# A top-2 mixture of experts computed from 128-token blocks of its chosen experts, in a fused four-layer kernel

## The chip, the cores and the metric

The program runs on one core of a Trainium2 chip. Its time is device microseconds for one execution of the whole program; three executions of the kernel before gave 5038.87 us as the median, with 5027.98 and 5039.68 at the ends. A change of the time counts here relative to that median.

## The reference, cut to what matters

The input `x` has 128 sequences of 32 tokens and 128 channels, so 4096 tokens. Twelve sublayers follow each other (L0 to L3, each a cross-attention, an attention and a feed-forward part), and each adds its result to `x`. The change is in the third one, the feed-forward part of L0, a mixture of eight experts:

```
x = x + _L0_ffn_ref(_layernorm(x, axis=-1), L0_ffn_w_router, L0_ffn_w_up, ...)
    logits = jnp.einsum('bsd,ed->bse', x, w_router)
    top_logits, idx = jax.lax.top_k(logits, K)                      # K = 2 of 8
    router_weights = jax.nn.softmax(top_logits, axis=-1)
    h = jnp.einsum('eud,bsd->bseu', w_up, x) + b_up[None, None]     # u = 512
    h = jax.nn.gelu(h, approximate=False)
    y = jnp.einsum('edu,bseu->bsed', w_down, h) + b_down[None, None]
    y_k = jnp.take_along_axis(y, idx[..., None], axis=2)
    out = jnp.einsum('bskd,bsk->bsd', y_k, router_weights)
```

The reference computes every expert for every token and then keeps two of the eight results of each token, weighted by a softmax of the two best router logits.

## The kernel before, in words

**Tiling.** The tokens are held in SBUF for the whole program as eight groups `X[0]` to `X[7]` of 512 tokens, each a tile of 128 partitions by 4 by 128 channels. All data are float32. Matmul results go to PSUM; ScalarE (ACT), VectorE (DVE) and GpSimd (POOL) work on them. The build fixes one order of instructions for each engine, close to the order in which the Python code emits them; at run time each engine goes through its list in sequence and stops at an instruction whose inputs or buffers aren't ready. The same holds for the queue of SyncE (SP), which issues nearly all the DMAs.

**The feed-forward part.** `L0_ffn` (L770) goes through the groups in chunks (0,1), (2,3), (4,5), (6), (7). For a chunk, `L0_ffn_chunk` (L783) normalizes the tokens, transposes them to `xT` (channels on partitions), computes the router's logits, takes maxima and their indices (L800, L801) and makes from them `R`, a weight of each of the eight experts for each token (`top_weights`; zero for the six experts not chosen). It adds the weighted `b_down` with the small matmuls `pbd`. Then, for each group and each of the eight experts, it computes all 512 tokens: four matmuls `pu` of 128x512 (L815), four Gelu activations into `Hh` (L816), sixteen matmuls `py` of 128x128 (L820), and `add_weighted` (L827), four vector instructions that add `R` times `py` to `X[g]`. That makes 64 passes of one expert over one group. The weights of all experts are in SBUF, in the tile `w_L_ffn`.

**Work beside it.** The attention part of L0 solves, for each token group, a batch of small 32x32 linear systems. It is spread over the neighbours of the feed-forward part by three queues of generators: `kq` builds the kernel matrices of a group (matmuls `kc`, results stored to DRAM as `phik` and `zd`), `sq` solves the systems on DVE (L702 and L703 load the matrices `A`, L707 to L726 eliminate; the result leaves as `yd`), and `oq` forms the output (L743 loads `Y`, then matmuls `ko`) and marks the group as ready for the feed-forward part. A fourth queue `dq` holds the whole of layer L1 for groups 0 and 1 (its own 16 experts have matmuls `ph` at L1087 and `py` at L1095). After each expert pass `side_steps(3, 5.5)` takes three steps of `kq`, 5.5 us worth of `sq`, and one step each of `oq` and `dq`. A chunk doesn't start before all of its groups are ready; the last solve, that of group 7, runs during the chunks (2,3) and (4,5). When the feed-forward part is done, the rest of `dq` is worked off, and the rest of L1 and L2 begins (`L2_xattn` of group 0 is its first part).

Of the kernel before, what the change touches and what calls it, by code (L numbers as in the profile page):

```python
# [9 lines left out]
FP = mybir.dt.float32  # L10
I32 = mybir.dt.int32
U32 = mybir.dt.uint32
AF = mybir.ActivationFunctionType
# [31 lines left out]
def _blocks(d):  # L45
# [18 lines left out]
                    ("temp", _rep(g(p + "temperature").reshape(1)))]  # L64
    p = "L0_ffn_"
    f["L0_ffn"] = [("wr", _kxm(g(p + "w_router"))),
                   ("wu", g(p + "w_up").transpose(2, 0, 1).reshape(128, -1)),
                   ("bu", g(p + "b_up").reshape(32, 128).T),
                   ("wd", g(p + "w_down").transpose(2, 0, 1).reshape(4, 128, 8, 128).transpose(1, 2, 0, 3).reshape(128, -1)),
                   ("bd", g(p + "b_down"))]  # L70
    for L in ("L1", "L3"):
        p = L + "_xattn_"
# [45 lines left out]
                  ("iota", _rep(np.arange(32))), ("pm", i[:, None] % 32), ("mh", np.full((128, 32), -0.5)),  # L118
                  ("hq", i[:, None] // 8 % 4 == np.arange(4)), ("km", i[:, None] // 32 == np.arange(32) // 8),
                  ("sel", (i[:, None, None] == 32 * np.arange(4)[:, None] + (i % 32)).reshape(128, -1)),  # L120
                  ("tm", (i[:, None] < 32) & (i[:, None] // 4 % 4 == np.arange(4)))]
    f["const"] = [(n, a.astype(np.float32)) for n, a in f["const"]]
    return f
# [11 lines left out]
def _host(inputs):  # L135

    d = {k: np.asarray(v) for k, v in inputs.items()}
    blocks = _blocks(d)
    arrays = {f"w_{n}": _pack(b) for n, b in blocks.items()}
    place = {}  # L140
    for n, b in blocks.items():
        at, place[n] = 0, {}
        for m, a in b:
            place[n][m] = (a.shape[0], at, a.shape[1])
            at += a.shape[1]
    arrays["x"] = np.ascontiguousarray(d["x"].reshape(4096, 128))
    arrays["ctx"] = np.ascontiguousarray(d["ctx_2048"])
    arrays["ctxT"] = np.ascontiguousarray(d["ctx_2048"].transpose(0, 2, 1))
    arrays["lens"] = np.ascontiguousarray(d["mask_BxS2_if0"])
    arrays["lidx"] = _rep(d["L0_attn_landmark_idx"])  # L150
    return arrays, place

# [13 lines left out]
class Kern:  # L166
# [85 lines left out]
    def run(self):  # L252
        nc = self.nc
        with self.pool("const") as const, self.pool("res") as res, self.pool("dram", 1, DRAM) as dram:
# [3 lines left out]
            self.rev, self.iota, self.pm, self.mh = cv["rev"], cv["iota"], cv["pm"], cv["mh"]  # L258
            self.hq, self.km = cv["hq"], cv["km"]
            self.sel, self.tm = cv["sel"], cv["tm"]  # L260
            self.X = []
            for g in range(NG):
                t = res.tile([128, 4, 128], FP, name=f"X{g}")
# [22 lines left out]
    def L0(self, W, es):  # L286
# [2 lines left out]
        self.qd = self.dram.tile([4096, 512], FP, name="phiq")  # L289
        self.zd = self.dram.tile([B, T, 144], FP, name="zd")  # L290
        self.yd = self.dram.tile([B, T, 144], FP, name="yd")
        self.kq, self.sq, self.oq, self.dq, self.ready = [], [], [], [], set()
        self.kps = es.enter_context(self.pool("kps", 2, PSUM, side="right"))
        with self.pool("sv", side="right") as self.sv, ExitStack() as self.es:
            self.L0_landmarks(W["L0_attn"])
            self.dq = [self.depool(self.es.enter_context(self.pool("dp", side="right")), self.kps, "m")]
            self.L0_xattn(W)
            wm = es.enter_context(self.pool("wm"))
            for n in ("L1_xattn", "L1_attn", "L1_ffn", "L2_xattn", "L2_attn"):
                W[n] = self.weights(wm, n, n)  # L300
            self.pa = es.enter_context(self.pool("pa"))
            self.A = self.L1_consts(W, self.pa)
            with self.pool("wf") as wf:
                W["L0_ffn"] = self.weights(wf, "L0_ffn", "L0_ffn")
                while self.kq:
                    self.side_steps(1, 8)
                self.L0_ffn(W["L0_ffn"], W)
                while self.dq:
                    self.side_steps(0, 0)
# [457 lines left out]
        self.ready.add(g)  # L767


    def L0_ffn(self, w, W):  # L770
        nc = self.nc
        wu = w["wu"].rearrange("p (e u) -> p e u", e=8)
        wd = w["wd"].rearrange("p (e k d) -> p e k d", e=8, k=4)
        with self.pool("fs", 2) as fs, self.pool("fr", 2) as fr, \
                self.pool("fpa", 3, PSUM) as fpa, self.pool("fpb", 3, PSUM) as fpb:
            for c in ((0, 1), (2, 3), (4, 5), (6,), (7,)):
                while not self.ready.issuperset(c):
                    self.side_steps(1, 6.5)
                self.L0_ffn_chunk(c, w, wu, wd, fs, fr, fpa, fpb)
                if c[0] == 0:  # L780
                    self.dq = [self.L1(g, W) for g in range(2)]

    def L0_ffn_chunk(self, c, w, wu, wd, fs, fr, fpa, fpb):  # L783
        nc = self.nc
        xT = fs.tile([128, 2, 512], FP, tag="xT")
        LG = fr.tile([128, 8, 8], FP, tag="LG")
        M8 = fr.tile([128, 8, 8], FP, tag="M8")
        I8 = fr.tile([128, 8, 8], U32, tag="I8")
        for q, g in enumerate(c):
            mv, rs = self.stats(fs, self.X[g], 4, 1e-5)  # L790
            xn = self.normed(fs, self.X[g], mv, rs)
            ps = fpa.tile([128, 512], FP, tag="a", name="pxt")
            self.transposed(ps, xn)
            nc.scalar.copy(xT[:, q, :], ps)
            ps = fpb.tile([128, 4, 8], FP, tag="b", name="plg")
            for i in range(4):
                nc.tensor.matmul(ps[:, i, :], lhsT=xT[:, q, i * 128:(i + 1) * 128], rhs=w["wr"], start=True, stop=True)
            nc.vector.tensor_copy(LG[:, 4 * q:4 * q + 4, :], ps)
            for i in range(4 * q, 4 * q + 4):
                nc.vector.max(M8[:, i, :], LG[:, i, :])  # L800
                nc.vector.max_index(I8[:, i, :], M8[:, i, :], LG[:, i, :])  # L801

        n = 4 * len(c)
        R = self.top_weights(fr, M8[:, :n], I8[:, :n], 2, 8, n)
        for q, g in enumerate(c):
            RT = self.weights_T(fpb, fs, R[:, 4 * q:4 * q + 4, :], 8)
            ps = fpb.tile([128, 4, 128], FP, tag="b", name="pbd")
            for i in range(4):
                nc.tensor.matmul(ps[:, i, :], lhsT=RT[:, i * 128:(i + 1) * 128], rhs=w["bd"], start=True, stop=True)
            self.addx(g, ps.rearrange("p i c -> p (i c)"))  # L810
            for e in range(8):
                Hh = [fs.tile([128, 512], FP, tag="Hh", name="Hh", bufs=6) for k in range(4)]
                for k in range(4):
                    ps = fpa.tile([128, 512], FP, tag="a", name="pu")
                    nc.tensor.matmul(ps, lhsT=wu[:, e, k * 128:(k + 1) * 128], rhs=xT[:, q, :], start=True, stop=True)  # L815
                    nc.scalar.activation(Hh[k], ps, AF.Gelu, bias=w["bu"][:, 4 * e + k:4 * e + k + 1])  # L816
                py = fpb.tile([128, 4, 128], FP, tag="b", name="py")
                for i in range(4):
                    for k in range(4):
                        nc.tensor.matmul(py[:, i, :], lhsT=Hh[k][:, i * 128:(i + 1) * 128], rhs=wd[:, e, k, :],  # L820
                                         start=k == 0, stop=k == 3)
                self.add_weighted(self.X[g], py, R[:, 4 * q:4 * q + 4, e:e + 1])
                self.side_steps(3, 5.5)

    def add_weighted(self, acc, ps, r):
        for i in range(4):
# [899 lines left out]
```

## Time and profile before

| What | Value |
|---|---|
| median of three runs (lowest, highest) | 5038.87 us (5027.98, 5039.68) |
| the execution that was profiled | 5026.48 us |
| its span, from first to last instruction | 5024.7 us |
| mean granted TensorE clock | 0.928 |
| first `pu` to last `py` of L0's feed-forward part | 2176.4 to 2813.8 us |
| bytes moved by DMA | 193.27 MB, 37 GB/s of HBM traffic over the span |

The profiled execution is the one whose stretches, chains and single instructions can be looked at; it lies 12.4 us below the median, so a difference worked out from its rows is added to 5026.48 for the execution and to 5038.87 for the median. PE is the matmul engine and PEld its weight load; "busy" is the time in which an engine executes, and an engine that waits is shown with the instruction that released it. PEclk is the clock that the chip granted to TensorE, as a share of full speed.

### The profile page before, as it was taken

The numbers are of one execution on the slowest core, as the hardware profiler recorded it, in microseconds if no ns is written. First come the engines' busy times: TensorE is split into PE (matmuls) and PEld (weight loads), VectorE is DVE, ScalarE is ACT, GpSimd is POOL, SyncE is SP. The second block draws the span as 40 slices with busy tenths as digits, with TensorE's granted clock in tenths as the row PEclk, the third lists the DMA queues.
The fourth block names the chain that finished last, engine by engine and source line by source line (L and its number), as shares of the span: only waits on it lengthen the run. The fifth ranks groups of instructions, "written<-read, shape, count | busy, mean of one in ns | idle before, by whom it ended". The sixth has DMA issues, their size and how long they took to land. (4 is left out here: it accounts for less than half of the span.)

```text
span 5024.7 us, 91248 instructions
## 1 busy us (share of the span) xinstructions
PE 4396.5 (87%) x34654; PEld 3147.0 (63%) x34654; DVE 3445.9 (69%) x10361; ACT 2388.4 (48%) x6481; POOL 1068.1 (21%) x1065
## 2 busy tenths in 40 slices
PE   7999898989898898879999888898888886879688
PEld 5777676767666676657766556565556653546455
DVE  5334959585867768582856689888888775777444
ACT  4555444454444445434444445454454554773233
POOL 1011111111111102121010122322322332322443
PEclk9999999999999999989999999999899987999677
DMA  4223141312222131323000001101010110000100
GB/s 138 61 60 56 43 67 38 63 47 56 47 54 53 49 60 41 51 74 40 1 12 3 27 27 28 28 26 29 25 28 28 37 42 19 1 1 14 38 13 11
DMA packets 354344, 193.27 MB, mean 38 GB/s; under 512 B 180065, under 2 KB 336481, under 8 KB 353265
## 3 DMA queue, kind: packets, MB, share of 16 engines
q1 hardware_dynamic: 353906, 187.45, 16.0%
q8 instruction: 273, 4.47, 0.4%
q14 instruction: 165, 1.35, 0.1%
HBM read 156.43 MB, written 30.96 MB: 37 GB/s over the span
## 5 line engine op out<-in xcount | busy, mean ns | idle before, releaser
L215 POOL TENSOR_TENSOR rs<-ve,w_const 128x4 f32<-128x4 f32 (+1 forms) x192 | 194.0, 1011 | 1706.2 <-DVE ve L213 1627.9
L541 PE MATMUL S<-cT,q 128*128 128x257 f32 x2048 | 535.4, 401 | 21.3 <-ACT E L545 21.0
L541 PEld LDWEIGHTS S<-cT,q 128*128 128x128 f32 x2048 | 386.6, 198 | 145.5 <-issue 57.8
L543 DVE TENSOR_REDUCE nm<-S 128x1 f32<-128x257 f32 x512 | 214.9, 420 | 367.5 <-PE S L541 365.7
L545 ACT ACTIVATE E<-S,nm 128x257 f32<-128x257 f32 x512 | 242.8, 475 | 362.3 <-DVE nm L544 361.3
L1180 PE MATMUL S<-cT,QM 128*128 128x289 f32 x1024 | 316.0, 427 | 74.7 <-ACT E L1182 69.8
L827 DVE SCALAR_TENSOR_TENSOR X<-py,R,X 128x128 f32<-128x128 f32 x768 | 223.6, 343 | 155.7 <-PE py L820 83.1
L1182 ACT ACTIVATE E<-S,nm 128x289 f32<-128x289 f32 x512 | 252.8, 498 | 153.6 <-DVE nm L1181 144.8
L820 PEld LDWEIGHTS py<-w_L_ffn,Hh 128*128 128x128 f32 x2048 | 259.6, 198 | 62.8 <-issue 40.3
L719 DVE TENSOR_TENSOR A<-A,elt 128x400 f32<-128x400 f32 (+22 forms) x608 | 295.6, 486 | 4.8
L524 PE MATMUL pq<-xT,WQK 128*128 128x128 f32 x2048 | 259.8, 284 | 36.1 <-ACT q L525 35.6
L717 DVE TENSOR_TENSOR elt<-A,row 128x400 f32<-128x400 f32 (+22 forms) x608 | 285.6, 470 | 8.0 <-DVE row L711 0.2
L580 PE MATMUL po<-TA,cN 128*128 128x512 f32 x512 | 274.9, 620 | 0.8 <-ACT TA L569 0.8
L1180 PEld LDWEIGHTS S<-cT,QM 128*128 128x128 f32 x1024 | 175.7, 194 | 158.5 <-issue 49.9
L524 PEld LDWEIGHTS pq<-xT,WQK 128*128 128x128 f32 x2048 | 244.8, 195 | 47.4 <-ACT q L525 43.7
L816 ACT ACTIVATE Hh<-pu,w_L_ffn 128x512 f32<-128x512 f32 x256 | 173.4, 686 | 212.6 <-PE pu L815 203.9
L820 PE MATMUL py<-w_L_ffn,Hh 128*128 128x128 f32 x2048 | 268.6, 284 | 3.7 <-ACT Hh L816 3.6
L581 PE MATMUL po<-TB,cN 128*128 128x512 f32 x512 | 267.6, 605 | 1.4 <-DVE TB L570 1.4
L555 ACT ACTIVATE E<-E,sm 128x256 f32<-128x256 f32 x512 | 218.4, 497 | 74.5 <-DVE sm L551 63.0
L815 PE MATMUL pu<-xT,w_L_ffn 128*128 128x512 f32 x512 | 247.6, 606 | 0.0
L1191 PE MATMUL pt<-w_const,E 128*96 128x128 f32 (+1 forms) x1536 | 233.2, 286 | 2.2 <-DVE ET L1194 1.9
L594 PE MATMUL pout<-WVO,OT 128*128 128x128 f32 x2048 | 234.2, 275 | 0.3 <-ACT OT L582 0.3
(471 smaller groups left out, 10204.7 us busy)
## 6 DMA issues: line engine op xcount, KB each, us to landing
cT<-ctxT SPq DMA_DIRECT2D x128, 257.0 KB
cN<-ctx SPq DMA_DIRECT2D x128, 256.0 KB
cT<-ctxT SPq DMA_DIRECT2D x32, 514.0 KB
phik<-PW SPq DMA_DIRECT2D x32, 256.0 KB
phiq<-P SPq DMA_DIRECT2D x32, 256.0 KB
A<-phik SPq DMA_DIRECT2D x128, 64.0 KB
PQ<-phiq SPq DMA_DIRECT2D x32, 256.0 KB
cN<-ctx SPq DMA_DIRECT2D x32, 194.0 KB
```

The source lines that it names most:

```text
L524: self.follow(st, nc.tensor.matmul(ps[:, k, :, :], lhsT=WQK[:, 4 * j + k, cb * 128:(cb + 1) * 128], rhs=t["x"], start=True, stop=True))
L541: self.follow(st, nc.tensor.matmul(S, lhsT=t["QP"][j][:, cb, b, :, :], rhs=t["cT"][b][:, cb, :], start=cb == 0, stop=cb == 1))
L545: nc.scalar.activation(E[:, j, 0:LK], S, AF.Exp, bias=m, accum_out=sm[:, j:j + 1])
L580: self.follow(st, nc.tensor.matmul(po, lhsT=cN[:, 0, c], rhs=TA, start=True, stop=False), nc.tensor.matmul(po, lhsT=cN[:, 1, c], rhs=TB, s ...
L581: nc.tensor.matmul(po, lhsT=cN[:, 1, c], rhs=TB, start=False, stop=True))
L594: self.follow(st, nc.tensor.matmul(po[:, 0, :], lhsT=OT[:, cb, h, :, :], rhs=WVO[:, cb, h, :], start=h == 0 and cb == 0, stop=False))
L717: nc.vector.tensor_tensor(t, A[:, k, :, i0:i1].rearrange("p h i -> p i h").unsqueeze(3).to_broadcast([128, m, HC, n]), row[:, :, i0:N].uns ...
L719: nc.vector.tensor_tensor(A[:, i0:i1, :, i0:N], A[:, i0:i1, :, i0:N], t, ALU.subtract)
L815: nc.tensor.matmul(ps, lhsT=wu[:, e, k * 128:(k + 1) * 128], rhs=xT[:, q, :], start=True, stop=True)
L820: nc.tensor.matmul(py[:, i, :], lhsT=Hh[k][:, i * 128:(i + 1) * 128], rhs=wd[:, e, k, :], start=k == 0, stop=k == 3)
L1180: self.follow(st, nc.tensor.matmul(S, lhsT=t["QM"][:, 0, 4 * j:4 * j + 4, :], rhs=t["cT"][:, b, :], start=True, stop=True))
L1182: nc.scalar.activation(E[:, j, :], S, AF.Exp, bias=nm[:, j:j + 1], accum_out=sm[:, j, b:b + 1])
```

## The change

Every token is computed only by its two experts. The groups are taken in four chunks of two groups, 1024 tokens, so 2048 pairs of a token and an expert. The pairs of an expert are put into blocks of 128 slots; since each expert may leave one block partly empty, 23 blocks always suffice, and 23 are always computed.

- **Front of a chunk** (`L0_ffn_front`, L863 of the changed file): normalization, transposes and logits as before. A new function `dispatch` (L781) works out, on DVE with two matmuls, the slot of each pair (`slot`) and, for each block, the rows of its expert's weights in DRAM (`rows`). Then 16 indirect DMAs on POOL's queue (`scatter`, L834) write the normalized tokens, 128 rows of 512 bytes each, to the DRAM tile `xsd[m]`. The weights of the two experts follow, and the part with `b_down`, as before.
- **Blocks** (`L0_ffn_blocks`, L911): for each of 23 blocks an indirect DMA on POOL's queue (`gather`, L837) brings the block's expert from the new DRAM array `l0e` to `wt`, 128 rows of 4112 bytes (`w_up`, `w_down` and `b_up` of the expert side by side), with four buffers. Every four blocks SP loads 512 slots (`xb`), and PE transposes them. A block is four matmuls 128x128 (`pu`), four Gelu of 128x128, and four matmuls 128x128 (`py`, delayed by one block); every four blocks ACT copies the results, and SP stores them to the DRAM tile `ysd[m]`. After each block comes `side_steps(2, 4.0)`. From block 10 on (counted from 0), the front of the next chunk is emitted as soon as its groups are ready.
- **Back** (`L0_ffn_back`, L955): 16 indirect gathers `G` (six buffers) bring each token's two results from `ysd[m]`, and 16 DVE instructions (L962) add them, weighted, to `X`. It is emitted after the next chunk's front and before the next chunk's blocks.
- **Start of the program**: a zero tile is written over the four `xsd` tiles by four DMAs on ACT's queue (L303), 1.507 MB each, since not every slot receives a token. The experts' weights leave the tile `w_L_ffn` of L0, which held them for the whole part.

In all, 64 scatters, 92 gathers of weights and 64 gathers of results stand on POOL's queue, 220 indirect DMAs; no indirect DMA was there before.

The core of the diff:

```diff
+        self.xsd = [self.dram.tile([23 * 128, 128], FP, name=f"xs{m}") for m in range(4)]
+        self.ysd = [self.dram.tile([23 * 128, 128], FP, name=f"ys{m}") for m in range(4)]
...
+            z = self.sv.tile([128, 128], FP, tag="z")
+            nc.gpsimd.memset(z, 0.0)
+            for m in range(4):
+                nc.scalar.dma_start(self.xsd[m].rearrange("(a p) c -> p a c", p=128), z.unsqueeze(1).to_broadcast([128, 23, 128]))
...
+    def scatter(self, dst, slot, src):
+        self.nc.gpsimd.indirect_dma_start(out=dst, out_offset=bass.IndirectOffsetOnAxis(ap=slot, axis=0), in_=src, in_offset=None)
+    def gather(self, dst, src, slot):
+        self.nc.gpsimd.indirect_dma_start(out=dst, out_offset=None, in_=src, in_offset=bass.IndirectOffsetOnAxis(ap=slot, axis=0))
...
     def L0_ffn(self, w, W):
-            for c in ((0, 1), (2, 3), (4, 5), (6,), (7,)):
-                while not self.ready.issuperset(c):
-                    self.side_steps(1, 6.5)
-                self.L0_ffn_chunk(c, w, wu, wd, fs, fr, fpa, fpb)
-                if c[0] == 0:
-                    self.dq = [self.L1(g, W) for g in range(2)]
+            chunks = ((0, 1), (2, 3), (4, 5), (6, 7))
+            st, old = None, None
+            for m, c in enumerate(chunks):
+                if st is None:
+                    while not self.ready.issuperset(c):
+                        self.side_steps(1, 6.5)
+                    st = self.L0_ffn_front(m, c, w, fs, fr, fpb)
+                if old:
+                    self.L0_ffn_back(*old, fs)
+                    if m == 1:
+                        self.dq = [self.L1(g, W) for g in range(2)]
+                new = None
+                for b, _ in enumerate(self.L0_ffn_blocks(st, fs, fpa, fpb)):
+                    self.side_steps(2, 4.0)
+                    if new is None and b >= 10 and m + 1 < 4 and self.ready.issuperset(chunks[m + 1]):
+                        new = self.L0_ffn_front(m + 1, chunks[m + 1], w, fs, fr, fpb)
+                st, old = new, st
+            self.L0_ffn_back(*old, fs)
...
+        slot, rows, OH = self.dispatch(fr, fpb, "b", I8, 8, 2, 8, 23)
+        for i in range(8):
+            for j in range(2):
+                self.scatter(self.xsd[m], slot[:, i, j:j + 1], XN[i // 4][:, i % 4, :])
...
+        for b in range(23):
+            wt = fs.tile([128, 1028], FP, tag="wt", bufs=4)
+            self.gather(wt, self.a["l0e"], rows[:, b:b + 1])
+            if b % 4 == 0:
+                n = min(4, 23 - b)
+                xb = fs.tile([128, 4, 128], FP, tag="xb")
+                nc.sync.dma_start(xb[:, 0:n, :], xv[:, b:b + n, :])
+                ...
+                self.transposed(ps, xb, n)
...
+            for k in range(4):
+                nc.tensor.matmul(ps[:, k, :], lhsT=wt[:, k * 128:(k + 1) * 128], rhs=xbT[:, b % 4 * 128:b % 4 * 128 + 128],
+                                 start=True, stop=True)
...
+                nc.scalar.activation(Hh[:, k, :], ps[:, k, :], AF.Gelu, bias=wt[:, 1024 + k:1025 + k])
...
+            for k in range(4):
+                nc.tensor.matmul(self.py[:, b % 4, :], lhsT=Hh[:, k, :], rhs=wd[:, k, :], start=k == 0, stop=k == 3)
+            if b % 4 == 3 or b == 22:
...
+                nc.scalar.copy(y[:, 0:n, :], self.py[:, 0:n, :])
+                nc.sync.dma_start(yv[:, b - n + 1:b + 1, :], y[:, 0:n, :])
...
+                G = fs.tile([128, 128], FP, tag="G", bufs=6)
+                self.gather(G, self.ysd[m], slot[:, i, j:j + 1])
+                nc.vector.scalar_tensor_tensor(x, G, E2[:, i, j:j + 1], x, ALU.mult, ALU.add)
```

`dispatch` is some 20 small DVE instructions on tiles of at most 128x184 elements: one-hot forms of the two chosen experts (`OH`), a running sum over the eight tiles of 128 tokens (`S`), one matmul with ones and one with a triangular matrix for the count of earlier pairs (`pdp`), the first block of each expert (`nb`, `end`), and from these `slot` and `rows`.

## The prediction, before the changed kernel ran

> **What bounds the kernel now.** I read the busy shares first, then the stage in which L0's feed-forward part runs (first `pu` 2176.4 us, last accumulation near 2815), its costliest groups, the spacing of its expert passes on DVE, and last the waits and single DMAs that resemble what the change adds.
>
> The page's first section, then the stage and two stretches of the start (columns: busy us and count of PE, PEld, DVE, ACT, POOL; then PEclk, DMA share, GB/s):
>
> ```profile
> PE 4396.5 (87%) x34654; PEld 3147.0 (63%) x34654; DVE 3445.9 (69%) x10361; ACT 2388.4 (48%) x6481; POOL 1068.1 (21%) x1065
> ...
> 2176.00:2815.00 639.00, 610.65 (x4122) 438.10 (x4122) 408.24 (x1432) 267.88 (x425) 59.05 (x52) 0.96 0.08 12
> ...
> 0.00:10.00 10.00, 0.00 (x0) 0.00 (x0) 0.59 (x3) 1.28 (x1) 1.19 (x6) 1.00 0.94 237
> 10.00:20.00 10.00, 0.00 (x0) 0.00 (x0) 6.40 (x13) 0.23 (x1) 0.00 (x0) 1.00 1.03 404
> ```
>
> The stage is bound by PE: 611 of 639 us. DVE has 408 us, POOL 59, DMA 8%. The program's first 20 us are the reverse: only DMA works.
>
> The stage's groups, and the accumulations of successive passes on DVE:
>
> ```profile
> L820 PE MATMUL py<-w_L_ffn,Hh 128*128 128x128 f32 x2048 | 268.6, 284 | 3.7 <-ACT Hh L816 3.6
> L815 PE MATMUL pu<-xT,w_L_ffn 128*128 128x512 f32 x512 | 247.6, 606 | 0.0
> L816 ACT ACTIVATE Hh<-pu,w_L_ffn 128x512 f32<-128x512 f32 x256 | 173.4, 686 | 212.6 <-PE pu L815 203.9 <-PE py L820 4.2
> L215 POOL TENSOR_TENSOR rs<-ve,w_const 128x4 f32<-128x4 f32 x19 | 19.7, 1039 | 218.2 <-DVE ve L213 186.3 <-DVE mv L198 19.9 <-DVE st L197 9.7
> ...
> 2369.15 1.13 DVE L827 SCALAR_TENSOR_TENSOR X<-py,R,X 128x128 f32<-128x128 f32 x4 [5.88 <-PE py L820]
> 2376.16 1.12 DVE L827 SCALAR_TENSOR_TENSOR X<-py,R,X 128x128 f32<-128x128 f32 x4 [5.88 <-PE py L820]
> 2383.17 1.13 DVE L827 SCALAR_TENSOR_TENSOR X<-py,R,X 128x128 f32<-128x128 f32 x4 [5.88 <-PE py L820]
> ```
>
> A pass costs 7.0 us of PE when nothing else runs, so the 64 passes are 448 us. It has 4 matmuls of 512 columns and 16 of 128, each twice in the counts (two passes): 8 x 512 + 32 x 128 = 8192 columns, 0.109 us for 128.
>
> The nearest DMAs to a DRAM round trip, in SP's timeline (start, duration of the issue):
>
> ```profile
> 2322.30 0.32 SPq L669 DMA_DIRECT2D phik<-PW  x1
> 2323.30 0.32 SPq L679 DMA_DIRECT2D zd<-Zs  x1
> 2324.32 0.58 SPq L702 DMA_DIRECT2D A<-phik  x1
> 2327.15 0.56 SPq L703 DMA_DIRECT2D A<-zd  x1
> ...
> 2528.42 5.27 SPq L732 DMA_DIRECT2D yd<-Yt  x8
> 2538.30 3.46 SPq L743 DMA_DIRECT2D Y<-yd  x2
> ```
>
> From the end of a store's issue to the load that waits for it: 1.7 us (`phik`), 3.5 (`zd`), 4.6 (`yd`).
>
> **What the change removes.** A block is 4 `pu`, 4 `py` and a share of one transpose, 17 counted passes of 128 columns with the halves: 1.85 us at full clock, so 92 blocks are 170 us of PE in place of 448: 278 us less. On DVE, 256 accumulations (75 us at 0.29 us spacing) go, 64 (20) and four dispatches (18) come: about 371 us stay. ACT's four 128x128 Gelus, at the 0.39 us of a 128x128 exponential in this trace, are 1.6 us a block, less than before. If only engines counted, the stage would end near DVE's 371 us, 240 us or more earlier.
>
> **What it adds, and where it stands.** All 220 indirect DMAs are on POOL's queue, in order. In the built program every scatter waits until the scatter before it has landed, since both write `xsd[m]`. So the 16 of a chunk form a chain, and behind a waiting scatter stand the weight gathers of the running chunk and the result gathers of the last one; PE waits for these. The `xb` loads on SP wait for all 16.
>
> No indirect DMA is in the trace. Its issue on POOL: from below the small POOL row, 1.0 us (L215: four elements take 1.04, so it is fixed cost); from above I allow 2.5. I take 1.5: more than the small row, since 128 addresses are to be worked out. Landing: from 1.7 (`phik`) to 4.6 (`yd`); I take 2.8, between `phik` and `zd`. A scatter in the chain is thus 4.3 us, bounds 2.7 and 7.1.
>
> Against this row stands a rule. The Trainium skill, "DMA: Bandwidth & Descriptors", section "Anatomy of one DMA — SWDGE (gpsimd) path", gives a DMA issued by GpSimd a fixed cost of about 2.0 us, nearly all of it the receipt of the write; with its 1 us to the first byte ("Latency and other measured facts") an estimate is 3.0 us for a scatter. The sum below has 57 exposed scatters: by the rule it is 57 x 1.3 = 74 us lower. I keep the rows, because the stores to DRAM in this very stage took 3.5 and 4.6 us, two of three above the rule. A second rule speaks the other way: "SBUF — State Buffer", section "SBUF: two separate sides", says that GpSimd cannot write descriptors while a VectorE instruction holds the port that both share. This trace shows such an interference once (a DVE TENSOR_SCALAR of 1.11 us at 2175.21 beside a POOL operation, usually 0.34). The solve's DVE instructions take up to 0.57 us: one such delay for each of 115 exposed indirect DMAs would be at most 65 us. I put 0.2 us each into the 1.5 and leave the rest to the range.
>
> A block when nothing is late: 2.7 us, not 1.85, because PE's clock falls in stretches with idle PE (PEclk 0.69 in 2120 to 2176) and because kernels and L1 run between. Its weights, 526 KB, take 1.3 us at 404 GB/s or 2.2 at 237, so they fit beside it with four buffers. In steps, from 2186 us, where the first routing indices are ready:
>
> - Chunk 0: dispatch 12, 16 scatters 69, the first `xb` 3: 84. PE has little else here.
> - Chunk 0, blocks 0 to 15: 43. Then the 16 scatters of chunk 1, among which stand the gathers of the last 7 blocks: 69.
> - Turn to chunk 1: 32 loads of `A` for the last solve stand on SP before the last `ys` stores and the first `xb` (22, at 0.63 each and a little), landing 10, ten gathers 15: 47.
> - Chunk 1, blocks 4 to 15: 32, and 10 for late slots. Then 13 scatters of chunk 2: 56.
> - Turn to chunk 2: `ys` landing 4, 16 gathers and 3 scatters 29, and 10 because `G` has six buffers and its DVE users stand among the last solve's steps: 43. Blocks 0 to 15: 43.
> - End of the last solve, `yd`, `Y`, output, front of chunk 3: 20. Of its scatters 12 exposed: 52. Turn to chunk 3: 34. Its last 19 blocks 51, its back 24 (16 x 1.5).
>
> Sum 608 us: end at 2794 instead of 2815, **-21**. The 278 us saved on PE come back as waits of the POOL chain (57 scatters 245, and 58 exposed gathers 87) and of SP.
>
> **What moves.** L1 of groups 0 and 1 runs in `dq`, one step for each call of `side_steps`. Before, its experts were done at 2855, some overlapping with L2's cross-attention, which starts at 2832. In the built order of the changed program L1 of group 1 is late: its experts all stand after chunk 3, beside L2's first part. Some 8 passes more than before are left: 18 us by their PE work (2.2 us each), 40 by the 5 us between two passes (`py` of L1 at about 2850 and 2855); I take **+29**. Its cover before was the solve's waits.
>
> **Start.** The zero fill writes 6.03 MB on ACT's queue ahead of the loads. DMA is 94% and 103% busy in the first 20 us, and PE starts at 20.32 on a weight load. At 237 GB/s it is 25 us, at 404 15 us; nothing if it falls behind the loads, 30 if the semaphores that it takes delay the `X` loads as well. I take **+22**. The gone 4 MB of weights came later, under cover: 0.
>
> In total -21 + 29 + 22 = **+30 us**: 5056.5 for a profiled execution (before 5026.5), 5069 for the median, which lies 12.4 above that execution.
>
> **Rivals.**
> - *Cheap indirect DMAs; faster.* The issue is 1.0 us (the POOL row) and the landing 1.7 (the `phik` row), a scatter 2.7: 57 x 1.6 = 91 and 58 x 0.5 = 29 less: 30 - 120 = -90, 4949 us. For it: the bounds are rows of this trace; PE and DVE together have room. Against: two of three stores landed slower. It decides once a scatter takes less than 4.3 - 30/57 = 3.8 us. By the skill's rule alone (3.0) the time is 4995.
> - *Dear indirect DMAs; slower still.* Issue 2.5, scatter 6.5: +125 and +58 on top, 5252. For it: DVE is 64% busy (408 of 639) and shares a port; against: the POOL row of 1.04 in the same stretch.
> - *The weights bound it.* 48.4 MB come in 92 pieces of 526 KB; if one took 3.3 us (160 GB/s) instead of less than 2.7, the 63 exposed blocks would add 38: 5107. The 404 GB/s of the start speak against it, but those are larger loads.
> - *The change doesn't cut the work,* because 23 blocks are too many: excluded, the counts in the code are fixed.
>
> **How the numbers follow.** A measurement tells about 0.3%, 15 us, from no change. Slower by more than that (my sum, the weights, dear DMAs): 0.62. Faster (cheap DMAs): 0.28. Within, a sum that comes out 15 to 45 us lower: 0.10. Prediction 5069 us. The range cuts the lowest tenth (cheap DMAs and hidden start, below 4935) and the highest (dear ones in full, above 5210). Within the slower case alone it is 5055 to 5210.
>
> **What would show it.** Right: POOL's scatters at 4.3 us spacing, `xb` loads released by the last of them, PE idle for 60 to 80 us at the start of chunk 0 and in each turn, first PE work near 42 us instead of 20, last feed-forward accumulation within 25 us of 2815 plus that shift. Wrong: scatters under 3.8 us apart; PE over 80% busy in the blocks; DMA as releaser of `pu` through the weight gathers; the start unmoved; or L1's tail no longer than before.

## The result, and the profile after

| | before | changed |
|---|---|---|
| median of four runs each (lowest, highest) | 5037.99 us (5027.98, 5039.68) | 5088.27 us (5074.16, 5096.12) |
| ratio to before, 95% interval | 1 | 1.0101 (1.0073 to 1.0128) |
| span of the profiled execution | 5024.7 us | 5072.1 us |
| mean granted TensorE clock | 0.928 | 0.895 |

The change made the kernel 1.0% slower, 50 us by the medians; the forecast was 30 us slower. The parts that make this up are others than forecast, as the profile shows. The profiled execution of the changed kernel is the fastest of its four (5074.16 us, 14 below their median), and that of the kernel before lies 12 below its own. First the page's busy shares and DMA queues of the changed kernel:

```profile
PE 4178.7 (82%) x33674; PEld 3047.8 (60%) x33674; DVE 3411.3 (67%) x10199; ACT 2340.2 (46%) x6638; POOL 1298.8 (26%) x1310
...
q0 software_dynamic: 17344, 56.83, 3.7%
q10 hardware_dynamic: 11840, 6.03, 0.4%
```

PE works 218 us less than before (4396.5 - 4178.7), POOL 231 us more. `q0` holds the indirect DMAs, `q10` the zero fill. So the work did go away; the time didn't. The stage by stretches (columns as before: busy us and count of PE, PEld, DVE, ACT, POOL, then clock, DMA share, GB/s):

```profile
2176.00:2851.00 675.00, 384.23 (x3048) 327.46 (x3048) 355.29 (x1220) 215.89 (x576) 285.85 (x287) 0.71 0.43 116
...
2178.00:2250.00 72.00, 12.74 (x48) 9.27 (x49) 63.73 (x248) 6.74 (x24) 28.98 (x31) 0.50 0.17 52
2250.00:2320.00 70.00, 60.58 (x538) 54.84 (x537) 23.96 (x99) 28.58 (x81) 28.22 (x33) 0.74 0.53 147
...
2380.00:2400.00 20.00, 0.00 (x0) 0.00 (x0) 0.00 (x0) 0.00 (x0) 0.00 (x0) 0.50 0.98 92
```

Over the whole stage no engine is busy for more than 57% of the time: PE 384 of 675 us, DVE 355. In the first stretch PE waits for the scatters of chunk 0. In the last one, from 2380 to 2400, nothing at all is computed: the `A` loads of the last solve and some weight gathers keep the DMA engines busy (share 0.98), and every engine waits. In the kernel before, the same loads ran under dense passes:

```profile
2340.00:2360.00 20.00, 18.50 (x108) 12.95 (x107) 9.39 (x59) 9.82 (x14) 1.02 (x1) 1.00 1.17 48
```

DMA was as full there (1.17, at 48 GB/s), and PE was busy for 18.5 of 20 us. That is the first hint at what the dense passes had been covering.

Now the scatters, in POOL's timeline of the changed kernel (start, duration; in brackets the idle time before it and the releaser):

```profile
2221.32 0.96 POOL L834 DMA_INDIRECT xs<-xn,slot  x1 [1.54 <-DMA xs<-xn,slot]
2223.81 0.96 POOL L834 DMA_INDIRECT xs<-xn,slot  x1 [1.53 <-DMA xs<-xn,slot]
2226.30 1.19 POOL L834 DMA_INDIRECT xs<-xn,slot  x1 [1.53 <-DMA xs<-xn,slot]
```

The view of the two source lines gives all of them (least, median and greatest ns, then the first and last start):

```profile
L834 POOL DMA_INDIRECT xs<-xn,slot x64: 952/1002/1773, 2197.6 to 2719.2; - x64
...
L837 POOL DMA_INDIRECT wt<-l0e,rows x92: 932/953/1710, 2199.1 to 2794.6; - x92
L837 POOL DMA_INDIRECT G<-ys,slot x64: 940/945/1599, 2403.8 to 2847.4; - x64
```

Here each scatter is released by the one before, as forecast; but a link is 2.5 us, 0.96 of issue and 1.53 of waiting, and a gather in a row is 1.25 (0.94 and a gap of 0.30). Nor does every scatter wait like this: later, gathers and other work of POOL stand between the scatters, and the time passes with them.

What stands still meanwhile is read from the waits of the stage (us in total, times, longest):

```profile
POOL wt L837 <- PE py L924: 120.6, 48, 12.0
PE pxb L230 <- DMA xb<-xs: 108.0, 4, 45.6
...
POOL xs L834 <- DMA xs<-xn,slot: 41.2, 29, 2.8
DVE p L716 <- DMA ys<-y: 39.8, 1, 39.8
...
POOL G L837 <- DMA ys<-y: 31.8, 3, 27.8
...
PE pu L943 <- DMA wt<-l0e,rows: 19.8, 15, 2.8
```

POOL's longest wait is not for scatters but for a free buffer of `wt`, which PE has still to read. PE waits for the first block's tokens at the start of chunks 0, 1 and 2 (45.6, 29.5 and 32.4 us; the fourth wait is 0.5). Only 29 scatters wait for the one before, 41.2 us in all. The fourth row is the first step of the last solve, at 2401 us, after 39.8 us of an idle DVE; it is put down to a `ys` store, but the loads of `A` end their issue at 2397, so these are the likelier releaser. The fifth is POOL, held for 27.8 us at the turn to chunk 1 by a `ys` store that stands on SP behind those loads. The last row says that the weights are no bound: PE waits for them 15 times, 19.8 us in all.

Following the work that comes last, by the start of its last instruction in each trace:

| last start of, us | before | changed | difference |
|---|---|---|---|
| L0's cross-attention (`pout`) | 2133.9 | 2136.3 | +2 |
| kernel matrices of group 7 (`kc`) | 2325.3 | 2360.9 | +36 |
| loads of `A` for group 7 (`A<-phik`) | 2348.3 | 2395.8 | +48 |
| last solve (`Yt`) | 2527.7 | 2582.9 | +55 |
| its output (`ko`) | 2565.5 | 2617.4 | +52 |
| experts of L1, group 0 (`u`) | 2705 | 2779 | +74 |
| experts of L1, group 1 (`u`) | 2851 | 2938 | +87 |
| experts of L1, group 7 (`u`) | 3889 | 3926 | +37 |
| cross-attention of L2 (`S`) | 4107.8 | 4144.4 | +37 |
| whole span | 5024.7 | 5072.1 | +47 |

The delay grows and shrinks along this column, and none of its first five rows is a product of L0's feed-forward part. The last 10 of the 47 us arise behind the last `S` of L2, where nothing was changed. The first part of L1 of group 0 starts within 5 us of the last `ko` in both kernels (2568.2 and 2622.4).

The rows for the last solve hide something. In the kernel before, its first step stands in DVE's list behind the additions of dense passes, 42 us after the last load of `A`:

```profile
2390.17 1.12 DVE L827 SCALAR_TENSOR_TENSOR X<-py,R,X 128x128 f32<-128x128 f32 x4 [5.88 <-PE py L820]
2391.22 0.15 DVE L707 TENSOR_SCALAR p<-A 128x2 f32<-128x2 f32 x1
```

In the changed kernel it comes right behind the loads:

```profile
2401.37 0.17 DVE L716 TENSOR_SCALAR p<-A 128x2 f32<-128x2 f32 x1 [39.83 <-DMA ys<-y]
```

So only 10 of the 48 us reach the start of the solve. The stretch of the solve, first before, then in the changed kernel, and in the latter DVE's additions of `G`:

```profile
2391.20:2528.00 136.80, 131.92 (x742) 95.79 (x741) 126.09 (x423) 58.55 (x109) 0.00 (x0) 0.98 0.00 1
...
2401.30:2583.00 181.70, 97.56 (x659) 88.86 (x659) 125.37 (x422) 59.90 (x198) 90.77 (x89) 0.73 0.46 141
...
L962 DVE SCALAR_TENSOR_TENSOR X<-G,E,X 128x128 f32<-128x128 f32 x32 | 11.1, 348 | 28.5 <-DMA G<-ys,slot 20.1 <-issue 8.5
```

DVE has as much to do in both (126 and 125 us), but the stretch is 45 us longer, and all of that is idle time: 28.5 us before the 32 additions of `G`, most of the rest before instructions that wait for PE, POOL and ACT.

### The profile page after: what moved, and what is told of

It is laid out like the page before. It is cut to its first block, busy times and chain, and to the rows that moved or that the text cites. A ratio compares the mean times of both kernels' runs of the same rounds, so it can differ in the third digit from the quotient of the medians.

```text
span 5072.1 us, 89808 instructions
## 1 busy us (share of the span) xinstructions
PE 4178.7 (82%) x33674; PEld 3047.8 (60%) x33674; DVE 3411.3 (67%) x10199; ACT 2340.2 (46%) x6638; POOL 1298.8 (26%) x1310
## 5 line engine op out<-in xcount | busy, mean ns | idle before, releaser
L240 POOL TENSOR_TENSOR QM<-QT,w_const 128x512 f32<-128x512 f32 x128 | 138.6, 1088 | 440.3 <-PE S L1319 429.3
L1320 DVE TENSOR_REDUCE nm<-S 128x1 f32<-128x289 f32 x512 | 219.0, 447 | 19.9 <-PE S L1319 16.8
L603 PEld LDWEIGHTS pout<-WVO,OT 128*128 128x128 f32 x2048 | 231.7, 192 | 0.9 <-ACT OT L591 0.5
L1330 PEld LDWEIGHTS pt<-w_const,E 128*96 128x96 f32 (+1 forms) x1536 | 181.3, 144 | 67.4 <-issue 44.6
L1651 ACT ACTIVATE E<-S,nm 128x128 f32<-128x128 f32 x512 | 180.1, 395 | 72.7 <-DVE nm L1648 72.7
```

Of the source, the lines that this page charges most:

```text
L603: self.follow(st, nc.tensor.matmul(po[:, 0, :], lhsT=OT[:, cb, h, :, :], rhs=WVO[:, cb, h, :], start=h == 0 and cb == 0, stop=False))
L1320: nc.vector.tensor_reduce(nm[:, j:j + 1], S, AX.X, ALU.max, negate=True)
L1330: self.follow(st, nc.tensor.transpose(pt[0:n, j * 128:(j + 1) * 128], E[:, j, k0:k1], self.ident))
```

## The experiments

Each kernel was timed beside the kernel before on the same chip; ratios are to it, with 95% intervals. "Below the changed kernel" compares with the 1.0101 above, which comes from four runs of each kernel in a session of its own.

### The zero fill alone

The kernel before, with this added at the start:

```diff
+            z = self.sv.tile([128, 128], FP, tag="z")
+            nc.gpsimd.memset(z, 0.0)
+            for m in range(4):
+                nc.scalar.dma_start(self.xsd[m].rearrange("(a p) c -> p a c", p=128), z.unsqueeze(1).to_broadcast([128, 23, 128]))
```

> The kernel before with one part of the change alone: the zero tile and the four DMAs on ACT's queue that write 6.03 MB over the xsd tiles at the start; nothing reads them. Theory A (the step of the prediction): +22 us, ratio 1.0044. Theory B (read from the profile of the changed kernel: first matmul at 32.38 us instead of 20.32, and the cross-attention still 9.3 us late at 1320 us): +9 to +12 us, ratio 1.002. Theory C (later waits swallow the delay): under +3 us, ratio 1.000.

Measured: 1.0034 (1.0021 to 1.0048), 17 us by the ratio, between A (1.0044, inside the interval) and B (1.002, just below it). In its own profile the first matmul is only 8 us later (28.4 instead of 20.3), and the last `pout` of the cross-attention, at 2136.0 us, only 2 us. So the late start does not account for the cost; where it arises no trace shows.

The other way round, the changed kernel with the fill moved off the start:

```diff
-            for m in range(4):
-                nc.scalar.dma_start(self.xsd[m]..., z...)
...
+                    if n in (20, 24, 28, 32):
+                        m = (n - 20) // 4
+                        nc.sync.dma_start(self.xsd[m].rearrange("(a p) c -> p a c", p=128), self.z.unsqueeze(1).to_broadcast([128, 23, 128]))
```

> The changed kernel with the four zero-fill DMAs moved from the start to SP's queue inside L0's cross-attention (at its sequences 20, 24, 28 and 32, where DMA is busy 10 to 30%). Theory A: 22 us back, 5066. Theory B: 9 to 12 us back, about 5078, ratio to before 1.008; first matmul at 20 us again. Theory C: nothing back, 5088.

Measured: 1.0054 (1.0039 to 1.0070), 0.47% or 24 us below the changed kernel's 1.0101. First matmul at 20.2 again. Two runs from two sides, 17 and 24 us: A's size was about right and the reading by the first matmul (B) too small.

### Without the chain of scatters

```diff
-                self.scatter(self.xsd[m], slot[:, i, j:j + 1], XN[i // 4][:, i % 4, :])
+                k = 2 * i + j
+                self.scatter(self.xsd[m] if k == 15 else self.xsn[m][k], slot[:, i, j:j + 1], XN[i // 4][:, i % 4, :])
```

> The changed kernel with the scatters of a chunk no longer chained: the first 15 go to a DRAM tensor each of its own, and only the last one to the tensor that the blocks read. This leaves most tokens out of the blocks, which compute rows of zeros in their place; the number of instructions and bytes is unchanged. Theory A (the chain of scatters on POOL sets the stage, as predicted): each of some 57 exposed scatters loses its wait of 1.53 us, 60 to 90 us less, 5000 to 5028, ratio 0.992 to 0.998. Theory B (the stage is set by the last solve, its loads on SP and what is behind them, and the chain is mostly beside it): 0 to 30 us less, ratio 1.004 or more.

Measured: 1.0060 (1.0040 to 1.0081), about 21 us below the changed kernel, with overlapping intervals: theory B. The chain did go: POOL's waits for a scatter to land are 0.3 us in the first stretch, and the first `pu` starts at 2222.8 instead of 2249.1. But the solve of group 6 ended 20 us later (2276.8 instead of 2256.9), the last `kc` 27 us later (2388 instead of 2361), and the last solve at 2586, no earlier than the 2583 of the changed kernel. The 26 us won at the start of chunk 0 were not on the path to it.

### The ys stores off SP's queue

```diff
-                nc.sync.dma_start(yv[:, b - n + 1:b + 1, :], y[:, 0:n, :])
+                nc.scalar.dma_start(yv[:, b - n + 1:b + 1, :], y[:, 0:n, :])
```

> The changed kernel with the ys stores issued on ACT's queue, right behind the copy that makes them, instead of SP's queue, where the last one of chunk 0 stands behind the 32 loads of A. Theory A (SP's order costs a turn of a chunk): POOL's wait of 27.8 us for the ys store (2376 to 2404 us) goes, the 16 gathers run in it, and the stage is 15 to 25 us shorter, 5063 to 5073. Theory B (the xb loads stand behind the same loads of A, so chunk 1 starts no earlier): under 5 us.

Measured: 1.0032 (1.0019 to 1.0045), 0.69% or 35 us below the changed kernel, more than A said. By the ratios, the place of one line's DMAs in a queue cost more than the scatter chain (35 and 21 us, though the intervals overlap a little). POOL's timeline shows the gathers 25 us earlier:

```profile
2372.03 0.94 POOL L837 DMA_INDIRECT wt<-l0e,rows  x1 [0.30 <-PE pxb L230]
2378.93 0.95 POOL L837 DMA_INDIRECT G<-ys,slot  x1 [5.96 <-issue]
2380.18 0.95 POOL L837 DMA_INDIRECT G<-ys,slot  x1 [0.31 <-issue]
```

They now run while `A` is loaded, and DVE adds all 16 of them ahead of the solve's first step (2385 to 2403.9 us; the last load ends its issue at 2398.8) instead of among its steps. The solve starts at 2404.6, 3 us later than in the changed kernel, and ends at 2568 instead of 2583. The experts of L1 end 16 us earlier; the two traces as a whole differ by 19 us, not by 35, because that of the changed kernel is its fastest run and this one lies 7 us above its median.

### Both moves, and the last chunk in two

> The changed kernel with both moves that gave time back alone: the zero fill inside the cross-attention (0.47% of before) and the ys stores on ACT's queue (0.69%). Theory A (they are independent, one at the start, one in a turn of a chunk): 1.0101 - 0.0047 - 0.0069 = 0.9985, no different from before. Theory B (what remains is set by POOL's chain, so one hides the other): 1.003 or more.

Measured: 1.0027 (1.0017 to 1.0037). B by its figure: the 0.47% and 0.69% do not add; with the stores moved, the late fill gives nothing that can be told. That POOL's chain hides it, as B says, this run doesn't show.

The chunk (6,7) is the last, and group 6 does not need the last solve. Split in two:

```diff
-            chunks = ((0, 1), (2, 3), (4, 5), (6, 7))
+            self.NB = (23, 23, 23, 15, 15)
+            chunks = ((0, 1), (2, 3), (4, 5), (6,), (7,))
```

> As the kernel with both moves, with the last chunk (6,7) taken as two chunks (6) and (7) of 15 blocks each, 99 blocks in place of 92 (so 7 blocks and their gathers more). Theory A (after the last solve the whole chunk (6,7) still has to be dispatched, scattered, computed and gathered, 200 us in the changed profile, of which group 6 needs no solve): with group 6 done beside the last solve some 60 to 100 us of that go, part of it is taken by L1's experts that are left over: 30 to 70 us less, ratio 0.985 to 0.992. Theory B (PE, POOL and the left-over experts fill that time anyway): 0 to 10 us less, ratio 0.997 or more.

Measured: 1.0023 (1.0012 to 1.0034), B: no difference from both moves alone that can be told.

> The changed kernel with that split of the last chunk alone, zero fill and ys stores as in the change. Theory A: 30 to 70 us less than the changed kernel, ratio 0.996 to 1.004. Theory B: ratio 1.008 or more.

Measured: 1.0027 (1.0016 to 1.0038), theory A, 37 us below the changed kernel. Alone, the split gives back as much as the stores did; with both moves it gives nothing more. Its trace shows what stands in the way: the first `S` of L2 starts at 2834.8 instead of 2870.1, but L1's experts of group 1 end at 2956 instead of 2938, and L2's last `S` is at 4128.3, where it is with the moves alone too (4129.3). Whatever was shortened before, the same line of L1 groups comes after.

The split with the 16 small loads of `A` put on ACT's queue:

> As the kernel with both moves and the split, with the 16 small loads of A (from zd) of each solve on ACT's queue instead of SP's, so that SP issues 16 in place of 32 before the first xb load of chunk 1. Theory A (the loads of the last solve, 37 us on SP in the changed profile, lie on the path to that solve): 10 to 15 us less. Theory B (the solve is paced by where its steps stand on DVE): under 5 us.

Measured: 1.0042 (1.0032 to 1.0052), neither theory: 0.2% worse, with intervals that overlap a little. The last load of `A` is issued 5 us earlier (2391.3 instead of 2396.1), but ACT's list has an order too: thirteen of these loads take it 14.9 us to issue, its Gelus stand behind them (14.4 us of an idle ACT), and the solve starts later (2416 instead of 2405).

### What the dense passes were worth

The question that all this raises can be put to the kernel before. Its passes of experts 3 to 7 are left out, and nothing is added:

```diff
             for e in range(8):
+                if e > 2:
+                    self.side_steps(3, 5.5)
+                    continue
```

> The kernel before, its dense loop kept, but with the matmuls, Gelus and accumulations of experts 3 to 7 left out (24 of 64 passes are computed, 168 us of PE in place of 448, about what the 92 blocks take); all 64 calls of side_steps stay, and no dispatch, scatter or gather is added. Theory A (the stage follows PE, so the change lost the gain in its own waits): 280 us less, ratio about 0.945. Theory B (behind the dense passes there is a chain that does not use them: kernel matrices of group 7, its loads, its solve, its output, then L1 of group 0, whose PSUM buffers come after those of that output, then the other groups of L1): the last ko stays near 2565 us and L1 of group 0 starts there, so only the 70 to 110 us of PE work that crowd the part behind it go, ratio 0.978 to 0.988.

Measured: 0.9869 (0.9846 to 0.9893): 66 us less, where 40 of 64 passes, 280 us of PE, are gone. This is theory B, and an estimate of the ceiling for a change that saves about these passes and leaves the work beside them where it is. The last `kc` (2346.6), the last solve (2532.4) and the last `ko` (2564.4) come no earlier than before (2325.3, 2527.7, 2565.5). The kernel before from 2400 to 2560:

```profile
2400.00:2480.00 80.00, 76.12 (x421) 54.16 (x420) 75.61 (x270) 33.20 (x64) 0.00 (x0) 0.97 0.01 1
2480.00:2560.00 80.00, 79.00 (x542) 59.84 (x542) 54.32 (x174) 32.79 (x56) 4.93 (x5) 0.98 0.08 15
```

and with 3 of 8 experts:

```profile
2400.00:2480.00 80.00, 17.57 (x114) 13.71 (x112) 66.38 (x184) 9.25 (x26) 0.00 (x0) 0.63 0.00 0
2480.00:2560.00 80.00, 9.04 (x108) 7.95 (x108) 53.80 (x167) 5.79 (x19) 5.06 (x5) 0.50 0.08 14
```

With 3 of 8 experts PE is busy for 27 of 160 us, while DVE, mostly at the last solve, has 120 us to do. In the full kernel PE was 97% busy there, with passes that did not set the end.

There is a second loss. After the last `ko` L1 goes expert by expert, a matmul between two DVE instructions. The row of that matmul among the groups from 2560 to 2860 us (busy us, mean ns), first before:

```profile
L1087 PE MATMUL ph<-xT,w_L_ffn 128*128 128x512 f32 x64 | 33.8, 610 | 0.0
```

then in the changed kernel:

```profile
L1226 PE MATMUL ph<-xT,w_L_ffn 128*128 128x512 f32 x34 | 21.6, 725 | 0.0
```

and with 3 of 8 experts:

```profile
L1090 PE MATMUL ph<-xT,w_L_ffn 128*128 128x512 f32 x58 | 43.3, 840 | 0.0
```

The same matmul takes 610, 725 and 840 ns in the mean (medians 595, 595 and 1021: in the changed kernel the fewer, slow ones raise it), and the 16 experts of group 0 take 72, 91 and 86 us from first to last. The granted clock goes with it. The window from 2640 to 2720 us in the kernel before:

```profile
2640.00:2720.00 80.00, 78.59 (x459) 57.51 (x458) 47.61 (x133) 28.39 (x45) 1.02 (x1) 1.00 0.00 1
```

in the changed kernel:

```profile
2640.00:2720.00 80.00, 51.13 (x308) 40.74 (x307) 43.23 (x136) 28.76 (x67) 47.79 (x47) 0.83 0.37 110
```

and with 3 of 8 experts:

```profile
2640.00:2720.00 80.00, 49.06 (x136) 27.69 (x135) 35.19 (x81) 8.81 (x14) 0.00 (x0) 0.58 0.03 8
```

PE was busy for 78.6 of 80 us at a clock of 1.00, for 51.1 at 0.83 and for 49.1 at 0.58. So the share of busy time alone doesn't give the clock. The Trainium skill, "TensorE: Matmul & The Clock Gate", section "Part 1: The HAM clock gate (the "warmup" mystery)", says that PE falls to half its clock after an idle window and needs a busy one to come back; the 0.50 of the idlest stretches above agrees. So with the passes that were saved beside this chain of single matmuls, its clock fell too. How much of the loss is the clock's no run separates.

### L1 with PSUM buffers of its own

L1's first part comes after the last `ko`, and the two share two PSUM buffers. In the kernel with both moves, L1 of groups 0 and 1 is given two of its own, one each from the pools of `pu` and `py`:

```diff
-                self.pool("fpa", 3, PSUM) as fpa, self.pool("fpb", 3, PSUM) as fpb:
+                self.pool("fpa", 2, PSUM) as fpa, self.pool("fpb", 2, PSUM) as fpb, self.pool("fl", 2, PSUM) as fl:
...
-                        self.dq = [self.L1(g, W) for g in range(2)]
+                        self.dq = [self.L1(g, W, fl) for g in range(2)]
```

> The kernel with both moves (zero fill in the cross-attention, ys stores on ACT's queue), with two PSUM buffers of their own for L1 of groups 0 and 1 (one taken from each of the pools of pu and py, three to two), in place of the two that they share with the output of the last solve. In the built order L1's experts of group 0 then stand before the last ko on PE, not behind it. Theory A (of the carry: idle PE of the stage can be used only if L1 isn't behind the last solve): L1 of group 1 is done near 2800 us instead of 2923, and 40 to 90 us go, ratio 0.985 to 0.995. Theory B (PE's idle time isn't usable, DVE or POOL bind): ratio 1.000 or more.

Measured: 1.0116 (1.0089 to 1.0144), B. The half of A that was about the place came true: L1's experts of group 0 end at 2641 us and of group 1 at 2826, 118 and 97 us earlier than with both moves alone. But the last solve now ends at 2650 instead of 2571 and the last `ko` is at 2698: the two share DVE, the solve's first step stands behind instructions of L1 there (2467 instead of 2406, with DVE busy for 31 of these 61 us), and the solve lost what L1 won. The sharing of buffers is why L1 starts where it does, but it had also kept L1's instructions out of the solve's way. What the smaller pools of `pu` and `py` cost was not separated.

> The same with the last chunk split into (6) and (7) as well, so that after the last solve only 15 blocks are left. Theory A: another 10 to 40 us less, ratio 0.978 to 0.990. Theory B: no more than 5 us apart from the one without the split.

Measured: 1.0077 (1.0053 to 1.0101); 20 us better than the last by the ratio, with overlapping intervals; the step is within A's 10 to 40, the ratio far above A's, and still behind both moves alone (1.0027).

### Dense where PE has nothing else to do

Groups 0 to 3 dense, groups 4 to 7 by blocks:

```diff
+                for c in ((0, 1), (2, 3)):
+                    ...
+                    for _ in self.L0_ffn_dense(c, w, fs, fr, fpa, fpb):
+                        self.side_steps(3, 5.5)
...
+            chunks = ((4, 5), (6,), (7,))
```

> Groups 0 to 3 by the dense loop of the kernel before (32 passes, weights in SBUF), groups 4 to 7 by blocks in chunks (4,5), (6) and (7): 53 blocks, 32 scatters and 32 gathers of results; zero fill (3.5 MB) inside the cross-attention, ys stores on ACT's queue. The dense passes take PE up to about 2565 us, where it had nothing else to do before the last solve is done (in the run with 3 of 8 experts PE was busy 27 of 160 us from 2400 to 2560); no scatter stands on POOL beside the kernel matrices of group 7 and its loads of A, which should then be as in the kernel before (last kc near 2325 us, Yt near 2530). Theory A (the price of the change is the delay of that chain): the gain behind the last solve stays and the delay goes, L1 of group 1 done near 2830 us, 20 to 60 us less than before, ratio 0.988 to 0.996, at best the 0.987 of 3 of 8 experts. Theory B (the turns between chunks cost as much wherever they are): ratio 1.000 or more.

Measured: 1.0096 (1.0080 to 1.0113), B. A's premise held: the last `kc` is at 2327.6, `Yt` at 2534.4, `ko` at 2570.5, within 7 us of the kernel before. Its conclusion didn't. The turn moved into the solve's stretch (PE waits 47 us for the scatters of chunk (4,5)), and behind the last `ko` L1's experts of group 0 end at 2733 and of group 1 at 2894, 28 and 42 us later than before, with blocks, gathers and a clock of 0.87 beside them. So the delay of the group 7 chain alone is not the cause either: what stands behind that chain was slower here, with blocks in place of dense passes, even though the chain was on time. Which part of these 42 us is the clock and which the DVE and POOL order was not separated.

No kernel tried here that does the whole work is faster than the one before; the best are 0.2 to 0.3% behind it.

## Why the prediction was right, and where it was not

The sign and the range were right: slower, 5088 in 4935 to 5210. The size was a little low (50 us, forecast 30). That it came so near is in good part luck, for two of the prediction's own signs of being wrong came true: the scatters were 2.5 us apart, and PE was over 80% busy in the first blocks (60.6 of 70 us from 2250 to 2320). Errors of both signs met in the sum: the stage came out longer than forecast, and what follows it lost less.

One reading behind the price of a scatter was wrong. In the 3.5 us between the store `zd` and the load that needs it, SP's queue of the kernel before holds another store, which waited for ACT (the second line is from SP's waits from 2318 to 2332 us):

```profile
2326.74 0.32 SPq L662 DMA_DIRECT2D phiq<-P  x1
...
SPq L662 <- ACT P L660: 1.8, 1, 1.8
```

These waits name no DMA at all, so neither the 1.7 nor the 3.5 us was a wait for a landing; of the three gaps only the 4.6 was.

Step by step:

- **"The stage is bound by PE."** This first reading failed, and it matters most. PE was 96% busy, yet 280 us of its work are worth 66 (3 of 8 experts). A busy share says that an engine has work at every moment, not that the end waits for it: the solve of group 7 and what follows it needed only some of that work. The ledger let 278 us "come back as waits of the POOL chain"; some 210 of them (278 less 66, an estimate) had never been there to gain.
- **Scatters.** Mis-sized: 4.3 us each, measured 2.5, and the sum exposed 57 of them (245 us), where 29 waited for the one before, 41 us in all. The rule that I set aside (3.0) was the nearer, and the rows that I kept were misread, as shown above. Gathers were 1.25, not 1.5.
- **The port of VectorE and GpSimd.** The solve's longest regular instructions take 0.74 us (128x560), not 0.57, so the bound of 65 us should have been 85. Neither was needed: all 220 indirect DMAs together took 18 us more than 220 times the shortest of them (0.93 us).
- **The faster rival.** Its condition came true, a scatter under 3.8 us, even under the 2.7 of its sum, and the kernel was still slower. So the rival's arithmetic failed with mine: both counted 57 exposed scatters at full price, and without any chain only about 21 us go.
- **The turns between chunks.** Right in kind: the loads of `A` on SP before the `ys` stores and `xb` loads were named, as 47 us in that turn. Moving the stores gave back 35. What I didn't see is that these loads had been hidden by dense passes and lay bare now. PE's waits at the starts of the chunks were 45.6, 29.5, 32.4 and 0.5 us, not 60 to 80.
- **The last solve.** I gave it 10 us for gathers among its steps. It ended 55 us later: its start moved by 10 and its length by 45 (136.5 to 181.5 us), 28.5 of them idle before additions of `G`. The kernel matrices of group 7 were 36 us late and the loads of `A` 48, but most of that was slack before, where the solve stood behind dense passes. Of the 36 not all belongs to the blocks: with 3 of 8 experts, where no block, scatter or gather was added, the last `kc` is 21 us late as well (2346.6), and with the first two chunks dense it is on time (2327.6). On POOL one case can be read: `Yb` of group 6, at 2288.17, stands behind weight gathers, of which the one at 2279.63 had waited 7.3 us for PE to free its buffer. There is a rival that no run tests: `side_steps(2, 4.0)` after each of 92 blocks hands out the work beside in other portions than `side_steps(3, 5.5)` after each of 64 passes. Which of these holds how much of the 36 was not separated.
- **Stage in sum.** Forecast -21; the last result was gathered near 2848, 34 us after the last pass of before.
- **L1's tail.** Forecast +29 at the end of the feed-forward part. It was +87 at the end of group 1, and six further groups won back 50, for a net 37. The order was as forecast: the experts of group 1 stand behind chunk 3, from 2858.8 us. But most of the delay came from further up: the experts of group 0 start 54 us late (2685.9 instead of 2631.4), behind the late `ko`; they take 19 us longer, at the lower clock; and 15 more go by before those of group 1.
- **Start.** The size was near, +22 forecast, 17 and 24 measured from two sides. The mechanism is not shown: the first matmul came 12 us later (32.4), not 22, and at the end of the cross-attention only 2 us are left of it. The agreement may be luck.

The parts do not sum by themselves: zero fill (24), stores (35) and split (37) each gave time back alone, and together hardly more than one of them (39 us). This is what several waits in front of one line of work would look like.

## What to carry to other kernels

Before costing an edit by the work that it saves, leave that work out and see what the kernel does: the run with 3 of 8 experts gave an estimate of the ceiling, 1.3%, and needed not a line of the dispatch. A busy engine may be busy with cover: list what runs under the work to be removed (here loads of small pieces, a long solve, kernel matrices), since each can become a wait of its own. And in a kernel with in-order queues look first at what a new DMA stands behind, and only then at what it costs.

## What the runs showed of the hardware that I had not expected

- An indirect DMA of 128 rows took POOL 0.95 to 1.0 us (medians) whether a row is 512 or 4112 bytes, and a scatter of 64 KB followed the one that it depends on 1.53 us after the end of its issue.
- TensorE's granted clock belongs to the neighbours' cost: 0.96 over the stage before, 0.71 with the change, and the same 128x512 matmul of L1 went from 610 to 725 ns in the mean (840 with 3 of 8 experts).
- In stretches that no change touched (from the last `S` of L2 to the last matmul of the program) the traces differ by up to 12 us: 913 us before, 923 in the changed kernel, 914 with both moves, 912 to 924 over all fourteen traces. A difference of that size between two single traces carries nothing.
